# Weighted rows in two column tiles and whole scores behind each quarter, in a two-layer cross-attention

## The chip, the core and the metric

The kernel runs on one core of one Trainium2 chip. All arithmetic is in fp32. The metric is the device time in microseconds (us) of one execution, as the median of several. A profiled execution gives a page and a trace, in which times are microseconds from the start of its span and TensorE's clock is the share that was granted.

## What is computed

Two layers of cross-attention act on x (8 batches of 100 rows and 1024 features). The keys and values of both come from the same context (8 batches of 1444 rows of 512 features). Cut to what matters, the reference is:

```python
# layer 0, for each batch
Q, K, V = x @ Wq + bq, ctx @ Wk + bk, ctx @ Wv + bv
w = softmax(Q @ K.T / 32, axis=keys)        # 100 x 1444
x = x + (w @ V) @ Wo + bo
# layer 1, for each batch
q, k, v = x @ Wq + bq, ctx @ Wk + bk, ctx @ Wv + bv
w = softmax(q @ k.T / 32, axis=queries)     # 100 x 1444
z = w @ v + x
out = (z - mean(z)) / sqrt(var(z) + 1e-6) * gamma + beta
```

## The kernel before, in words

The products are regrouped. Instead of keys, the kernel forms the product of the query and key weights (`weight_products`), applies it to x (`queries`, giving gT: 512 context features by 400 columns for four batches) and multiplies by the context itself. Instead of values, it weights the context's rows first (`weighted_rows`) and applies the value weights afterwards (`project0`, `project1`, `project_last`). Many of the large products are done in Strassen-like form, with sums on the other engines.

For each batch of each layer there are then two products with the context:

- `scores` (line 921): 100 queries by 1444 context rows, with 512 features to sum over in `LC` = 4 chunks of 128. A chunk of gT (128 x 100) is the stationary operand, that of the transposed context `cT` (128 x 1444) moves. The result lies in `NB` = 4 PSUM banks. With `alone=True` the 1444 columns are cut into 4 pieces of 361 columns, one a bank; otherwise into `NP` = 11 pieces of 131 or 132, three to a bank. The function is a generator: each `next` issues one matmul, and the last of them also issues the evictions by ScalarE (line 945) and as much of the softmax as belongs there.
- `weighted_rows` (line 898): 512 context features by 100 queries, with the context rows to sum over in `MC` = 12 chunks of 120 (the last has 124). A chunk of context rows `c` by 128 features is the stationary operand, the chunk's weights `w` (120 x 100) move, and the four blocks of 128 features lie side by side in one PSUM bank of 400 columns. That is 48 calls a batch, with 4 for each chunk; each `next` issues one.

An fp32 matmul call appears in the trace as two weight loads (LDWEIGHTS, engine PEld) and two matmuls (engine PE).

`alternated` (line 1292) joins the two: for batch b it loads the rows of b in four parts and the features of b + 2 in four chunks, and then issues a step of A (the weighted rows of b) and one of s (the scores of b + 2) in turn, until both are used up: 48 of A and 44 of s. Batches 6 and 7 have no scores to run beside. The loads are issued by SP's queue, in order, into the `stream` pool of ten buffers; a buffer is filled again when its last reader has ended.

The order on TensorE is that of the program (`manual_schedule(engines={PE})`), so the main loops set it:

- Scores of batches 0 and 1 come alone in each layer (`first_scores`, 16 calls each).
- Layer 0 (loop at line 1310): batches 0 to 5 are alternated. In batches 6 and 7 parts of projection 0 (`o0`) are put in behind every fourth step of A.
- Layer 1 (loop at line 1374 and on): batches 0 to 7 in the sets 0 to 3, 4 to 6 and 7, with `project1` behind the first two. `finish` transposes finished rows back with one transpose behind a step of A, eight to a batch (`untransposed`, line 1183); the table `finished` starts it at steps 2, 16 and 30 of batch 4, 34 of batch 5, and 2, 15 and 28 of batch 7. `weight_totals` (line 1147) puts two transposes behind one step of batches 1, 3, 5 and 7.

The softmax of layer 0 runs along the rows and is then transposed on VectorE (16 STREAM_TRANSPOSE instructions); that of layer 1 transposes first and then takes maxima, exponentials and sums by groups of four chunks. Both make the weights `w` that A of the same batch reads, one batch later than the scores' own.

Of the kernel before, what the change touches and what calls it, by code (L numbers as in the profile page):

```python
# [29 lines left out]
PE = mybir.EngineType.PE  # L30

P = 128
B, T, E = 8, 100, 1024
S, L = 1444, 512
EC, LC = E // P, L // P
NQ = 4
MC, MR = 12, 120
MX = S - MC * MR
QR = MR * MC // NQ
CQ = MC // NQ  # L40
GM = 4
NP, PM = 11, 3
NB = -(-NP // PM)
QD = 32
SW = (MC - 1) * MR + P
PT = 4
# [9 lines left out]
def two_layer_cross_attention(ctx: ExitStack, tc: tile.TileContext, a: dict, out: bass.AP):  # L56
    nc = tc.nc
# [10 lines left out]
    def bank(name):  # L68
        return psum.tile([P, 512], F32, tag="ps", name=name)

    def bank2(name):
        return psum2.tile([P, 512], F32, tag="ps2", name=name)

    def unit(name):
        return stream.tile([P, E + L], F32, tag="unit", name=name)

    def wide(name):
        return work.tile([P, LC, GT], F32, tag="AT", name=name, bufs=2)

# [3 lines left out]
    def weight_rows(name):  # L83
        return work.tile([P, MC * T + QD * (-(-T // QD)) - T], F32, tag="wT", name=name, bufs=3)
# [35 lines left out]
    quarter = const.tile([P, P // QD], F32, tag="quarter", name="quarter")  # L120
# [747 lines left out]
    def load_features(b):  # L868

        for k in range(LC):  # L870
            t = unit(f"cT_{b}_{k}")[:, :S]
            nc.sync.dma_start(out=t, in_=a["ctxT"][b][k * P : (k + 1) * P, :])
            yield t

    def load_rows(b):

        src = a["ctx_512"][b]
        for q in range(NQ):
            t = unit(f"c_{b}_{q}").rearrange("p (c l) -> p c l", c=CQ)
            n = CQ - (q == NQ - 1)  # L880

            rows = bass.AP(src.tensor, src.offset + q * QR * L, [[L, P], [MR * L, n], [1, L]])
            nc.sync.dma_start(out=t[:, :n, :], in_=rows)
            if n < CQ:
                m = (MC - 1) * MR
                for r0, r1 in ((0, 112), (112, MR + MX)):
                    nc.sync.dma_start(out=t[r0:r1, n, :], in_=src[m + r0 : m + r1, :])
            yield t
# [5 lines left out]
    def held(c):  # L894

        return MR + (MX if c == MC - 1 else 0)

    def weighted_rows(w, c, dst, name):

        ps = bank2(name)  # L900
        for m in range(MC):
            r = held(m)
            for k in range(LC):
                nc.tensor.matmul(  # L904
                    ps[:, k * T : (k + 1) * T],
                    c[m // CQ][:r, m % CQ, k * P : (k + 1) * P],
                    w[:r, m, :],
                    start=(m == 0 and k == 0),
                    stop=(m == MC - 1),
                    skip_group_check=True,  # L910
                )
                if (m, k) == (MC - 1, LC - 1):
                    src = ps[:, :GT].rearrange("p (c t) -> p c t", t=T)
                    if name.startswith("A1"):
                        nc.scalar.copy(dst, src)
                    else:
                        nc.vector.tensor_copy(dst, src)
                yield


    def scores(s, layer, cT, softmax, alone=False):

        b = s["b"]
        p = s["p"] = prob[b % len(prob)][:T, :S]
        q = gT[layer][b // G]
        t0 = b % G * T
        n_pieces, per = (NB, 1) if alone else (NP, PM)
        cuts = [S * n // n_pieces for n in range(n_pieces + 1)]
        banks = [bank(f"s{layer}_{b}_{n}") for n in range(NB)]
        for k in range(LC):  # L930
            for n in range(n_pieces):
                o = cuts[n // per * per]
                nc.tensor.matmul(  # L933
                    banks[n // per][:T, cuts[n] - o : cuts[n + 1] - o],
                    q[:, k, t0 : t0 + T],
                    cT[k][:, cuts[n] : cuts[n + 1]],
                    start=(k == 0 and n % per == 0),
                    stop=(k == LC - 1),
                    skip_group_check=True,
                )  # L940
                if (k, n) != (LC - 1, n_pieces - 1):
                    yield
        parts = [slice(cuts[n * per], cuts[min((n + 1) * per, n_pieces)]) for n in range(NB)]
        for part, ps in zip(parts, banks):
            nc.scalar.activation(  # L945
                p[:, part],
                ps[:T, : part.stop - part.start],
                AF.Identity,
                bias=key_bias[layer][:T, b : b + 1],
                scale=SCALE,  # L950
            )
        w = s["rows"] = weight_rows(f"w{layer}_{b}")
        s["w"] = w[:, : MC * T].rearrange("p (c t) -> p c t", t=T)

        s["softmax"] = softmax(s, parts)
        for _ in islice(s["softmax"], LATER.get((layer, b))):
            pass
        yield
# [318 lines left out]
    batches = [{"b": b} for b in range(B)]  # L1277
    A0 = [wide(f"A0T_{g}") for g in range(2)]

    def loaded(*loads):  # L1280

        got = [[] for _ in loads]
        for _ in range(NQ):
            for load, to in zip(loads, got):
                to.append(next(load))
        return got
# [5 lines left out]
    def alternated(b, layer, softmax, dst):  # L1292

        nxt = b + 2 < B
        c, *cT = loaded(load_rows(b), *([load_features(b + 2)] if nxt else []))
        A = weighted_rows(batches[b]["w"], c, dst, f"A{layer}_{b}")
        ahead = scores(batches[b + 2], layer, *cT, softmax) if nxt else iter(())
        for _ in range(MC * LC):
            next(A)
            next(ahead, None)  # L1300
            yield

    key_bias = [c0, None]
# [6 lines left out]
    for b in range(B):  # L1310
        steps = alternated(b, 0, softmax0, A0[b // G][:, :, b % G * T : (b % G + 1) * T])
        if b == B - 2:
            o0 = project0(AS, A0)
        if b < B - 2:
            run(steps)
        else:

            more = next(o0)
            if b == B - 1:
                gT[1], queries1 = queries(1, wqk1, u1)  # L1320
            for n, _ in enumerate(steps):
                if n % 4 == 3 and n > 4:
                    next(more, None)
                    if b == B - 1 and n < 16:
                        next(queries1)
        for e in range(2 * b, 2 * b + 2) if 2 * b < EC else ():
            add_out_bias(e)
        if b == 0:
            sums = quarter_sums("k1")
            block_sums("u1", acc_u, sums[:, :LC, :], late=True)  # L1330
            block_sums("wqbk1", acc_c, sums[:, LC : LC + EC, :], late=True)
        if b == 1:
            got = totals("k1", sums[:, : LC + EC, :], LC + EC)
            u1, wqbk1 = got[:, :LC], got[:, LC:]
            vector.in_order = True
            AS = value_sums(wvo)
            vector.in_order = False
# [36 lines left out]
    for bs in SETS:  # L1374
        t = wide(f"A1T_{bs[0]}").rearrange("p c t -> p (c t)")[:, : LC * len(bs) * T]
        t = t.rearrange("p (c t) -> p c t", c=LC)
        for i, b in enumerate(bs):
            for n, _ in enumerate(alternated(b, 1, softmax1, t[:, :, i * T : (i + 1) * T])):
                if b % 2 and n == (8 if b == B - 1 else 27):
                    weight_totals(batches[b - 1 : b + 1])  # L1380
                if (b, n) in finished:
                    finishing.append(finish(batches[finished[b, n]]))
                finishing = [f for f in finishing if next(f, finishing) is not finishing]
            if b == 1:
                AS = project1_sums(wv1)
        if b == B - 2:
            first = last_columns(wv1)
        if b < B - 1:

            between, room = {3: (batches[5], (0, 3, 3, 3, 3)), 6: (batches[7], (1, 0, 0, 1, 2))}[b]  # L1390
            project1(bs, *AS, t, between["softmax"], room)
# [26 lines left out]
```

## Time and profile before

| | us |
|---|---|
| time, median of 2 runs | 632.83 (632.43 to 633.23) |
| profiled execution: span, which is the only time the page gives for it | 630.5 |
| busy: PE / PEld (of the span) | 621.6 (99%) / 534.7 (85%) |
| busy: DVE / ACT / POOL | 474.2 / 179.5 / 97.7 |
| A: matmul records / load records, 1536 of each | 249.8 / 218.0 busy |
| s of both layers: matmul records, 1184 | 245.6 busy |
| mean granted clock of TensorE | 0.997 |

PE's busy time counts the matmuls and PEld's the weight loads that overlap them. Records of consecutive matmuls overlap as well, since each is shown with its way through the array, so the busy time of a group is less than its count times its mean; the rate is read from the starts, or from the chain of waits, whose pieces do not overlap.

The stages in order of time: weight products and queries to 183; first scores to 203; layer 0's batches with scores to 321; its batches 6 and 7 to 350; projection 0, queries of layer 1 and its first scores to 436; layer 1's batches 0 to 3 to 515, `project1` to 534, batches 4 to 6 to 588, `project1` to 602, batch 7 and the end to 630.5.

### The profile page before, as it was taken

The page shows a single profiled execution, that of the slowest core. Times are in us where ns is not written, and L with a number is a line of the kernel's source. Part 1 is how long each engine was busy: PE and PEld are TensorE (multiplying, and loading weights), DVE is VectorE, ACT ScalarE, POOL GpSimd, SP SyncE. Part 2 cuts the span into 40 slices and gives each one's busy share as a digit, 9 for nine tenths or more (in the row PEclk, how much of TensorE's full clock was granted, in tenths as well). Part 3 has the DMA queues.
Part 4 walks back from the last instruction along what each step waited for, and adds up shares of the span by engine and source line. Part 5 has one row for each costly group of instructions (what it writes and reads, how often), then busy time and mean ns, then how long its engine had stood idle before and what let it go on. Part 6 is the DMA issues. An engine that isn't in the chain of part 4 may idle for free.

```text
span 630.5 us, 10617 instructions
## 1 busy us (share of the span) xinstructions
PE 621.6 (99%) x4142; PEld 534.7 (85%) x4142; DVE 474.2 (75%) x990; ACT 179.5 (28%) x406; POOL 97.7 (16%) x141
## 2 busy tenths in 40 slices
PE   9999999999999999999999999999999999999995
PEld 8886467688986999999989666756999999999992
DVE  2987688896875797666658686968777659887885
ACT  1323123314304234423230001113433240338303
POOL 3110111112230000000000002108111220423042
PEclk9999999999999999999999999999999999999998
DMA  8969989636999889998942309856889890697414
GB/s 273 295 147 320 306 220 333 120 80 117 206 326 388 269 311 293 329 313 313 298 161 86 104 0 337 268 195 192 298 298 309 309 315 26 198 289 282 124 24 83
DMA packets 54959, 144.35 MB, mean 229 GB/s; under 512 B 4732, under 2 KB 10108, under 8 KB 54908
## 3 DMA queue, kind: packets, MB, share of 16 engines
q1 hardware_dynamic: 46462, 119.63, 54.9%
q0 software_dynamic: 8048, 23.57, 17.9%
q8 instruction: 33, 0.54, 0.4%
q10 hardware_dynamic: 398, 0.47, 0.2%
q14 instruction: 18, 0.15, 0.1%
HBM read 123.36 MB, written 6.14 MB: 205 GB/s over the span
## 4 chain that ended last, share of the span: by engine, by line
PE 97%; issue 1%; ACT 0%; POOL 0%; DVE 0%; DVEq 0%; POOLq 0%; ACTq 0%
PE s L933 25%; PE A L904 25%; PE qk_x L163 7%; PE g_x L163 5%; PE o_x L163 5%; PE vo_x L163 3%; PE o_y L163 3%; PE g_y L163 3%; PE qk_y L163 2%; PE qk_z L163 2%; PE o_z L163 1%; PE o_w L163 1%; PE qk_w L163 1%; PE vo_y L163 1%; PE vo_z L163 1%; PE z L1198 1%
## 5 line engine op out<-in xcount | busy, mean ns | idle before, releaser
L904 PE MATMUL A<-w,c 120*128 120x100 f32 (+1 forms) x1536 | 249.8, 265 | 0.0
L904 PEld LDWEIGHTS A<-w,c 120*128 120x128 f32 (+1 forms) x1536 | 218.0, 190 | 2.8
L96 DVE STREAM_TRANSPOSE w<-prob 32x384 f32<-32x384 f32 (+1 forms) x256 | 143.7, 561 | 27.6 <-ACT prob L972 9.7
L933 PE MATMUL s<-cT,g1T 128*100 128x131 f32 (+2 forms) x592 | 122.9, 296 | 0.0
L933 PE MATMUL s<-cT,g0T 128*100 128x131 f32 (+2 forms) x592 | 122.7, 296 | 0.0
L933 PEld LDWEIGHTS s<-cT,g1T 128*100 128x100 f32 x592 | 78.4, 167 | 8.6 <-issue 0.3
L933 PEld LDWEIGHTS s<-cT,g0T 128*100 128x100 f32 x592 | 78.2, 167 | 8.4 <-PE c L599 0.4
L945 ACT ACTIVATE prob<-s,c 100x393 f32<-100x393 f32 (+2 forms) x64 | 34.7, 559 | 112.6 <-PE s L933 99.4
L1121 ACT ACTIVATE w<-w,negmax 120x100 f32<-120x100 f32 (+1 forms) x96 | 34.8, 365 | 82.6 <-DVE negmax L96 82.6
L965 DVE TENSOR_REDUCE maxima<-prob 100x1 f32<-100x394 f32 (+3 forms) x32 | 16.5, 528 | 24.3 <-ACT prob L945 24.0
L1362 POOL DMA_DIRECT2D wv<-in_L_xattn_Wv x1 | 0.8, 777 | 192.8 <-PE o_x L163 192.8
L163 PE MATMUL qk_x<-qk 128*128 128x256 f32 x128 | 30.0, 382 | 0.0
L1140 POOL TENSOR_TENSOR part<-w 120x500 f32<-120x500 f32 x8 | 10.9, 1366 | 118.5 <-DVE rstd L1213 28.6
L163 PEld LDWEIGHTS qk_x<-qk 128*128 128x128 f32 x128 | 23.6, 193 | 3.0 <-ACT qk L437 0.2
L675 ACT ACTIVATE g1T<-g_x,k 128x400 f32<-128x400 f32 x4 | 2.4, 594 | 68.9 <-PE g_x L163 68.7
L1121 ACT ACTIVATION_READ_ACCUMULATOR w<-w,negmax 120x1 f32 (+1 forms) x96 | 18.0, 187 | 0.0
L96 DVE TENSOR_TENSOR xT<-xT,o_x 128x400 f32<-128x400 f32 (+1 forms) x32 | 15.8, 538 | 2.2 <-PE o_x L163 2.0
L1202 DVE SCALAR_TENSOR_TENSOR z<-vectors,r,z 100x512 f32<-100x512 f32 x16 | 11.8, 740 | 6.3 <-PE z L1198 6.3
L1198 PE MATMUL z<-ident,xT 128*100 128x128 f32 x64 | 16.3, 273 | 0.0
L163 PE MATMUL vo_x<-vo 128*128 128x512 f32 x32 | 15.3, 595 | 0.0
L969 ACT ACTIVATE prob<-prob,negmax 100x1444 f32<-100x1444 f32 x8 | 12.0, 1498 | 11.2 <-DVE negmax L967 11.2
L96 DVE TENSOR_TENSOR w<-w,rtotal 120x400 f32<-120x400 f32 (+1 forms) x24 | 14.1, 586 | 0.7
(433 smaller groups left out, 987.8 us busy)
## 6 DMA issues: line engine op xcount, KB each, us to landing
cT<-in_ctxT SPq DMA_DIRECT2D x64, 722.0 KB, 6.8
c<-in_ctx SPq DMA_DIRECT2D x48, 768.0 KB, 7.6
c<-in_ctx SPq DMA_DIRECT2D x16, 512.0 KB, 8.0
vo<-in_L_xattn_Wo SPq DMA_DIRECT2D x8, 512.0 KB, 7.7
qk<-in_L_xattn_WqT SPq DMA_DIRECT2D x8, 512.0 KB
qk<-in_L_xattn_WqT SPq DMA_DIRECT2D x15, 256.0 KB, 5.8
c<-in_ctx SPq DMA_DIRECT2D x16, 224.0 KB, 6.4
xT<-in_xT SPq DMA_DIRECT2D x2, 1600.0 KB
```

Source lines behind the costliest of these rows:

```text
L96: ins = getattr(nc.vector, op)(*args, **kw)
L163: nc.tensor.matmul(banks[n // per][:, n % per * width : (n % per + 1) * width], lhs[i][:, n * P : (n + 1) * P], rhs[i], start=(fresh and i ...
L675: nc.scalar.activation(dst[g][:, c, :], banks[j][:, :GT], AF.Identity, bias=u[:, c : c + 1])
L904: nc.tensor.matmul(ps[:, k * T : (k + 1) * T], c[m // CQ][:r, m % CQ, k * P : (k + 1) * P], w[:r, m, :], start=(m == 0 and k == 0), stop=( ...
L933: nc.tensor.matmul(banks[n // per][:T, cuts[n] - o : cuts[n + 1] - o], q[:, k, t0 : t0 + T], cT[k][:, cuts[n] : cuts[n + 1]], start=(k == ...
L945: nc.scalar.activation(p[:, part], ps[:T, : part.stop - part.start], AF.Identity, bias=key_bias[layer][:T, b : b + 1], scale=SCALE,)
L965: nc.vector.tensor_reduce(maxima[:, n : n + 1], p[:, part], AX.X, ALU.max)
L969: nc.scalar.activation(p, p, AF.Exp, bias=negmax, accum_out=total)
L1121: nc.scalar.activation(w[:r, m0 + m, :], w[:r, m0 + m, :], AF.Exp, bias=negmax[:r, m : m + 1], accum_out=total[:r, m : m + 1])
L1140: add(part, w[:MR, 0:5, :], w[:MR, 5:10, :], ALU.add)
L1198: nc.tensor.transpose(ps[:T, e * P : (e + 1) * P], xT[:, 4 * j + e, b * T : (b + 1) * T], ident)
L1202: nc.vector.scalar_tensor_tensor(z[:, half], bv1[j][:T], s["r"], ps[:T, :], ALU.mult, ALU.add)
```

## The change

In `weighted_rows` each matmul of 128 features becomes two of 64. The first writes PSUM partitions 0 to 63 and the second 64 to 127 of the same columns, with the same moving operand. The columns of the array that a matmul uses follow the partitions that it writes, so the two are column tiles. The weighted rows have 96 calls a batch in place of 48; a `next` issues two.

In `alternated` the scores are taken with `alone=True` (16 calls of 361 columns in place of 44 of 131 or 132), and they are not issued one for each step of A: behind steps 11, 23, 35 and 47 come four calls, which are one feature chunk over all four pieces. The sixteenth `next` issues the last matmul, the evictions and the start of the softmax, at step 47; before, that came at step 43.

```diff
+HP = P // 2
...
         for m in range(MC):
             r = held(m)
             for k in range(LC):
-                nc.tensor.matmul(
-                    ps[:, k * T : (k + 1) * T],
-                    c[m // CQ][:r, m % CQ, k * P : (k + 1) * P],
-                    w[:r, m, :],
-                    start=(m == 0 and k == 0),
-                    stop=(m == MC - 1),
-                    skip_group_check=True,
-                )
+                for h in range(2):
+                    nc.tensor.matmul(
+                        ps[h * HP : (h + 1) * HP, k * T : (k + 1) * T],
+                        c[m // CQ][:r, m % CQ, k * P + h * HP : k * P + (h + 1) * HP],
+                        w[:r, m, :],
+                        start=(m == 0 and k == 0),
+                        stop=(m == MC - 1),
+                        skip_group_check=True,
+                    )
...
         A = weighted_rows(batches[b]["w"], c, dst, f"A{layer}_{b}")
-        ahead = scores(batches[b + 2], layer, *cT, softmax) if nxt else iter(())
-        for _ in range(MC * LC):
+        ahead = scores(batches[b + 2], layer, *cT, softmax, alone=True) if nxt else iter(())
+        quarter = MC * LC // NQ
+        for n in range(MC * LC):
             next(A)
-            next(ahead, None)
+            if n % quarter == quarter - 1:
+                for _ in range(NB):
+                    next(ahead, None)
             yield
```

## The prediction

> **What bounds the kernel now.** The page comes first: is one engine busy throughout, and does the chain that ended last run on it?
>
> ```profile
> span 630.5 us, 10617 instructions
> PE 621.6 (99%) x4142; PEld 534.7 (85%) x4142; DVE 474.2 (75%) x990; ACT 179.5 (28%) x406; POOL 97.7 (16%) x141
> ...
> PE 97%; issue 1%; ACT 0%; POOL 0%; DVE 0%; DVEq 0%; POOLq 0%; ACTq 0%
> ...
> L904 PE MATMUL A<-w,c 120*128 120x100 f32 (+1 forms) x1536 | 249.8, 265 | 0.0
> L904 PEld LDWEIGHTS A<-w,c 120*128 120x128 f32 (+1 forms) x1536 | 218.0, 190 | 2.8
> ```
>
> TensorE is the path: 97% of the chain, and no idle time before its matmuls. Every fp32 matmul of the program is two records (768 calls, 1536 records of A), each with its own weight load. A busy PE does not say whether matmuls or loads set the pace, so the next view is busy time by stage, over four batches of the weighted rows A with the scores s: two of layer 0, two of layer 1.
>
> ```profile
> core 0: us, PE busy (x) PEld busy (x) DVE busy (x) ACT busy (x) POOL busy (x), PEclk, DMA share, GB/s
> ...
> 262.40:282.10 19.70, 19.70 (x187) 19.70 (x186) 12.04 (x24) 7.04 (x9) 0.00 (x0) 1.00 0.94 322
> 282.10:301.70 19.60, 19.60 (x186) 19.60 (x185) 11.94 (x24) 7.04 (x9) 0.00 (x0) 1.00 0.90 302
> ...
> 476.00:495.60 19.60, 19.60 (x186) 19.60 (x185) 12.86 (x26) 7.16 (x30) 3.60 (x7) 1.00 0.92 314
> 495.60:515.30 19.70, 19.70 (x186) 19.70 (x185) 12.82 (x26) 7.07 (x29) 3.62 (x7) 1.00 0.89 301
> ```
>
> Matmuls and weight loads are both busy without a gap, at the full clock: a load runs while the matmul ahead of it streams, and the longer of the two sets each step. How long is a step? The timeline inside a batch:
>
> ```profile
> 539.66 0.36 PE L904 MATMUL A<-w,c 120*128 120x100 f32 x2
> 539.86 0.39 PE L933 MATMUL s<-cT,g1T 128*100 128x131 f32 x2
> 540.09 0.36 PE L904 MATMUL A<-w,c 120*128 120x100 f32 x2
> 540.28 0.39 PE L933 MATMUL s<-cT,g1T 128*100 128x131 f32 x2
> 540.51 0.36 PE L904 MATMUL A<-w,c 120*128 120x100 f32 x2
> ```
>
> A takes 0.20 us from its start to the next start, s 0.23, a pair 0.43. Last the chain of waits, where its pieces show both kinds alone and the steps that prices are taken from.
>
> ```profile
> 73.62 6.87 PE vo_x L163 x16
> ...
> 395.84 5.37 PE g_x L163 x16
> ...
> 426.62 9.73 PE s L933 x32
> ...
> 494.57 1.09 PE A L904 x10
> ...
> 576.35 11.59 PE A L904 x104
> ```
>
> A alone takes 0.111 a record (11.59/104), 0.222 a step. Matmuls whose moving side is wide follow their width: 400 columns 0.336 (5.37/16), 512 columns 0.429 (6.87/16), so 0.83 ns a column, and s in pieces of 361 columns 0.304 (9.73/32), as that slope gives. So 100 columns stream in 0.336 - 300 x 0.00083 = 0.087, and A alone, at 0.111, is held by the load of its 128 columns. In the pair, A's 0.20 is 0.111 for its own second load and 0.087 for the 100-column load of s. Loads of 128 and 100 columns in 0.111 and 0.087 give 0.056 for 64.
>
> **The change, part by part.** (1) *Scores in wide pieces.* Per batch 44 calls of 131 columns become 16 of 361: 32 records x 0.304 = 9.73 us. Their 0.087 loads hide behind 0.304 of streaming.
>
> (2) *Weighted rows in halves.* A step of two records becomes four, each with a 64-column load and the same 100 moving columns: the halves share neither. No row of this trace shows an output of 64 partitions or two matmuls in the array at once, so the step is bounded: 2 x 0.087 = 0.174 if both halves stream and load side by side; 4 x 0.087 = 0.348 if they go one after another; between them, 4 x 0.056 = 0.224 if the streams overlap and the loads stay in one file. I take 0.224, nearest to the row that sets A's pace today, a load queue that is never idle.
>
> Twelve batches have scores beside them (0 to 5 of each layer); each takes 19.63 now (by the chain: one ends at 262.44, the next at 282.07). New: 48 x 0.224 + 9.73 = 20.48, so +0.85 each, +10.2. Four batches are A alone: 4 x 48 x (0.224 - 0.222) = +0.4.
>
> (3) *Changes of the array's shape.* Scores, transposes and projections stay at full width, so every passage from halves to them or back is a change. Alternated batches: 2 layers x 6 x 4 quarters x 2 = 96. Layer 0, batches 6 and 7: the chain shows 8 and 7 insertions of projection 0, 30, and 2 at the ends. Layer 1: the transposes of `finish` follow single A steps; 24 in batch 4, two of them behind scores, 22 x 2 = 44; 8 in batch 5, one behind scores, 14; 24 in batch 7, 48; three weight totals between A steps, 6; entry and exit of batches 6 and 7, 4. In all 244. No row has such a change. The lower bound is 0 (a transpose between A steps costs 0.11 today, its load and nothing more). The upper is an emptied array and an uncovered load: an A matmul lasts 0.264 of which 0.087 is streaming, leaving 0.177; a load lasts 0.190 where 0.111 is its pace, so 0.079 + 0.056 = 0.135 for a half; together 0.31. I take 0.09, the middle of 0 and 0.177 with the load hidden: 244 x 0.09 = +22.0. The ends are 0 and +76.
>
> *Trainium skill, against this change.* The trace has loads running under matmuls of the same rows (19.70 of 19.70 busy on both). "TensorE: Matmul & The Clock Gate", Part 3, The mechanism, says that a load overlaps matmuls in flight only where its row group differs; two column halves have the same rows. By that rule a step would be 4 x (0.056 + 0.087) = 0.572 and the time 911; by the trace's rows it stays 0.224 and the sum below. "TensorEngine Tiling (Array Packing)", Overview and Key Properties, recommends tiles for dimensions of at most 64, where these are 128 features that fill the array, and says that a change of tiling mode drains TensorE; it gives no figure, and no row here shows one. The same page says tiles load and multiply in parallel, which would be the 0.174.
>
> (4) *What hides at nothing.* Scores end with the last A step, not 4 steps (0.9 us) before it, and the last eviction is 0.56, so the softmax starts 1.1 to 1.4 later. Its layer 1 chain, the longer:
>
> ```profile
> 475.57 9.46 DVE L96 STREAM_TRANSPOSE w<-prob 32x384 f32<-32x384 f32 x16 [4.15 <-POOL wsum L1145]
> ...
> 490.43 0.57 DVE L96 TENSOR_TENSOR w<-w,rtotal 124x400 f32<-124x400 f32 x1
> ```
>
> The weights are ready at 491.0 and A needs them at 495.4 (494.57 + 8 records): 4.4 of cover, 3.0 after the shift, 1.5 if batches also shrink by 1.5. Uncovered, it would cost its excess in each of 12 batches. SP's queue issues the same DMAs in the same order. A row tile is freed up to 2.4 earlier (a quarter's scores now come behind it), a feature tile at 25, 50, 75 and 100% of the batch against 23, 46, 69 and 92%; the ten-buffer rotation reuses each about one batch before it is read, 19.6 against 6.8 to 8 us to landing. POOL's queue is not touched. The four score banks are now taken at the first scores call, n = 11, not n = 0, when those before have been evicted.
>
> **Sum.** 630.5 + 10.2 + 0.4 + 22.0 = 663.1 of span. The page gives no time beside its span; the median of the two runs is 632.83, 2.3 above it, and I add that: 665.
>
> **The rivals.** *Side by side and free (the other side).* Step 0.174: 12 x (8.35 + 9.73 - 19.63) = -18.6; A alone 192 x -0.048 = -9.2; each of the 122 runs of A starts and ends with one half alone, 122 x 0.087 = +10.6. Sum -17.2: 615.6 with free changes. For it: halves share no column and no partition of the result. Against: 218 us of A's loads in one unbroken file. It is faster only while a change costs under 17.2 / 244 = 0.07; over 2% only under 0.02. *Side by side, changes at 0.02 to 0.12, or loads in file and changes nearly free:* 620 to 645 (the latter 643 at 0). *One after another.* That is the case in which the change does not do what it says: step 0.348, 12 x 6.80 + 192 x 0.126 = +105.8, so 739 with free changes, 761 at 0.09, 783 at 0.177. For it: in every row of the trace matmuls start no closer than their stream or load allows. Against: each half uses other columns. *Softmax late* adds at most its excess and needs 3 us more; no time of its own.
>
> **How the numbers follow.** Two per cent, 12.7 us, is about what a measurement of this kernel can tell from no change: 620.2 and 645.5. Side by side and free (615 to 620) 0.18; cheap changes (620 to 645) 0.19; the forecast with changes at 0.01 to 0.23 (646 to 700) 0.37; one after another (739 to 783) 0.23; still dearer 0.03. Faster 0.18, same 0.19, slower 0.63. The forecast's own range is 646 to 700; the eight in ten reach from 615 to 760, leaving out the dearer half of the serial case, the 0.03 and a little below.
>
> **What would show it.** Step (1): 32 s records of 0.30 in a batch. Step (2): starts of A inside a quarter, 12 steps in 2.1, 2.7 or 4.2 us. Step (3): the time between the last A and the first s of a quarter over what their streams need, and the same at a transpose. Step (4): no wait of A for w. The prediction is wrong if the step lies below 0.2 or above 0.25, or a change outside 0 to 0.23.

## The result, and the profile after

The changed kernel takes 641.88 us (641.67 to 642.1, 2 runs) against 632.83: a ratio of 1.0145, 95% interval 1.0129 to 1.0162. The profiled execution spans 639.9 us, 9.4 more than before. It is slower, as forecast, but by 9 us and not by 32; by the two per cent that the prediction takes as its measure it counts as no change, though the interval is clear of 1. The page after, first the busy times, then the chain that ended last and the groups of A:

```profile
span 639.9 us, 12346 instructions
PE 630.7 (99%) x5006; PEld 451.8 (71%) x5006; DVE 476.2 (74%) x990; ACT 180.0 (28%) x406; POOL 98.7 (15%) x141
...
PE 77%; issue 8%; DVE 6%; ACT 4%; POOL 4%; POOLq 0%; DVEq 0%; ACTq 0%
...
L906 PEld LDWEIGHTS A<-w,c 120*64 120x64 f32 (+1 forms) x3072 | 135.2, 137 | 39.1 <-issue 26.3
L906 PE MATMUL A<-w,c 120*64 120x100 f32 (+1 forms) x3072 | 159.0, 253 | 0.3 <-issue 0.3
```

TensorE is still busy throughout. The chain that ended last gives it less (77%, before 97%): from 493 us on it is followed back over the softmax and the normalisations, with one piece of 26.9 us in which the engine waited for nothing that the profile shows, so it does not tell what bounds the kernel there. TensorE's own waits do. They are 1.7 us in all, one of them in A:

```profile
PE warm L109 <- DVE ones L106: 1.1, 1, 1.1
PE g_z_x L164 <- DVE qk L97: 0.3, 1, 0.3
PE A L906 <- issue: 0.3, 1, 0.3
```

But A's matmuls, twice as many, are busy for 159 us and not 250, and the weight loads are no longer one file without a gap (71%, before 85%). So A itself became much faster, and something else took the time back. Which stage? Busy time by stage, after:

```profile
203.26:319.05 115.79, 115.79 (x1348) 80.44 (x1347) 84.38 (x167) 38.86 (x51) 0.00 (x0) 1.00 0.93 316
319.05:348.72 29.67, 29.67 (x416) 21.43 (x415) 20.87 (x45) 3.71 (x5) 0.00 (x0) 1.00 0.25 79
...
531.97:591.76 59.79, 59.46 (x675) 39.99 (x675) 42.12 (x79) 23.73 (x71) 17.00 (x22) 1.00 0.73 228
...
606.31:624.57 18.26, 18.26 (x221) 12.20 (x221) 12.06 (x20) 2.34 (x3) 5.68 (x8) 1.00 0.15 23
```

and the same stages of the kernel before:

```profile
202.98:321.32 118.34, 118.34 (x1111) 118.34 (x1110) 84.61 (x169) 39.55 (x52) 0.00 (x0) 1.00 0.89 304
321.32:350.32 29.00, 29.00 (x222) 26.67 (x221) 20.09 (x43) 3.09 (x3) 0.00 (x0) 1.00 0.30 96
...
534.26:587.94 53.68, 53.68 (x500) 53.68 (x500) 45.30 (x84) 23.70 (x71) 16.71 (x22) 1.00 0.80 254
...
602.25:615.28 13.03, 13.03 (x125) 13.03 (x124) 11.14 (x20) 1.15 (x1) 5.53 (x8) 1.00 0.22 33
```

Layer 0's batches with scores gained 2.55 us, its batches 6 and 7 lost 0.67, layer 1's batches 0 to 3 gained 0.85 (78.94 to 78.09). The loss is in two stages, batches 4 to 6 of layer 1 (+6.11) and batch 7 (+5.23): those with the transposes of `finish` between steps of A. The rest of the span differs by 0.8 in all. Inside a batch of layer 0, the timeline after:

```profile
266.05 2.28 PE L906 MATMUL A<-w,c 120*64 120x100 f32 x48
268.26 2.68 PE L935 MATMUL s<-cT,g0T 128*100 128x361 f32 x8
270.87 2.28 PE L906 MATMUL A<-w,c 120*64 120x100 f32 x48
273.08 2.68 PE L935 MATMUL s<-cT,g0T 128*100 128x361 f32 x8
275.69 2.28 PE L906 MATMUL A<-w,c 120*64 120x100 f32 x48
```

A quarter is 2.21 us of A (from its start to that of s) and 2.61 of s, 4.82 together and 19.28 a batch; before, 19.63. Where transposes stand between single steps, the timeline after and then the one before, both from batch 7:

```profile
606.91 0.32 PE L1200 MATMUL z<-ident,xT 128*100 128x128 f32 x1
607.16 0.39 PE L906 MATMUL A<-w,c 120*64 120x100 f32 x4
607.48 0.32 PE L1200 MATMUL z<-ident,xT 128*100 128x128 f32 x1
```

```profile
602.74 0.28 PE L1198 MATMUL z<-ident,xT 128*100 128x128 f32 x1
602.85 0.36 PE L904 MATMUL A<-w,c 120*128 120x100 f32 x2
603.05 0.27 PE L1198 MATMUL z<-ident,xT 128*100 128x128 f32 x1
```

A transpose and a step of A take 0.57 where they took 0.31.

What the halves do is seen in single starts. The trace does not name the half of a record; that is read from the order and the spacing of the starts. It has, in microseconds, at the start of the first run of A above and around the scores ahead of it:

```
A, two records at a time  266.186 266.192   266.271 266.278   266.357 266.364   ... 86 ns from pair to pair
last pair of a run        263.256 263.263
load for s                263.441    second record of s 263.826, so the first streams from about 263.522
last record of s          265.654    it streams to about 265.958
loads of the next A       266.047 266.054    second pair 266.186, so the first streams from about 266.100
```

Two records start 6 to 7 ns apart, every 86 ns: 0.172 a step, the stream of 100 columns and nothing else. I take the two to be of different halves, since records of one half start 86 ns apart ("Half by half", below). And at a change of shape nothing is loaded for 0.09 us after the last stream has ended (0.088 to 0.092 at all 93 edges between A and scores), and then a load that was hidden lies open (0.08 for 100 columns, 0.05 for 64). A run of A costs its steps and two changes: 2.21 - 12 x 0.172 = 0.15 and 2.61 - 8 x 0.304 = 0.18, 0.32 with rounding.

### The profile page after: what moved, and what is told of

The parts are those of the page before. It is cut to its first block, busy times and chain, and to the rows that moved or that the text cites. A ratio compares the mean times of both kernels' runs of the same rounds, so it can differ in the third digit from the quotient of the medians.

```text
span 639.9 us, 12346 instructions
## 1 busy us (share of the span) xinstructions
PE 630.7 (99%) x5006; PEld 451.8 (71%) x5006; DVE 476.2 (74%) x990; ACT 180.0 (28%) x406; POOL 98.7 (15%) x141
## 4 chain that ended last, share of the span: by engine, by line
PE 77%; issue 8%; DVE 6%; ACT 4%; POOL 4%; POOLq 0%; DVEq 0%; ACTq 0%
PE s L935 21%; PE A L906 15%; PE qk_x L164 7%; PE g_x L164 5%; DVE w L97 5%; PE vo_x L164 3%; PE o_x L164 3%; PE g_y L164 3%; PE qk_z L164 2%; PE qk_y L164 2%; POOL rstd L1216 1%; PE o_y L164 1%; ACT z L1218 1%; ACT w L1123 1%; PE qk_w L164 1%
## 5 line engine op out<-in xcount | busy, mean ns | idle before, releaser
L906 PEld LDWEIGHTS A<-w,c 120*64 120x64 f32 (+1 forms) x3072 | 135.2, 137 | 39.1 <-issue 26.3
L906 PE MATMUL A<-w,c 120*64 120x100 f32 (+1 forms) x3072 | 159.0, 253 | 0.3 <-issue 0.3
L935 PE MATMUL s<-cT,g1T 128*100 128x361 f32 x256 | 84.2, 474 | 0.0
L935 PE MATMUL s<-cT,g0T 128*100 128x361 f32 x256 | 84.1, 474 | 0.0
L947 ACT ACTIVATE prob<-s,c 100x361 f32<-100x361 f32 x64 | 34.4, 561 | 104.8 <-PE s L935 90.4
L935 PEld LDWEIGHTS s<-cT,g1T 128*100 128x100 f32 x256 | 40.5, 166 | 31.5 <-issue 0.3
L935 PEld LDWEIGHTS s<-cT,g0T 128*100 128x100 f32 x256 | 40.3, 166 | 31.3 <-PE c L600 0.4
L967 DVE TENSOR_REDUCE maxima<-prob 100x1 f32<-100x361 f32 x32 | 16.4, 527 | 11.3 <-ACT prob L947 9.9
L1218 ACT ACTIVATE z<-z,rstd 100x1024 f32<-100x1024 f32 x7 | 8.0, 1149 | 30.2 <-POOL rstd L1216 30.2
L1216 POOL TENSOR_TENSOR rstd<-rstd,mhalf 100x1 f32<-100x1 f32 x7 | 9.8, 1393 | 43.1 <-DVE rstd L1215 43.1
```

Source lines behind the costliest of these rows:

```text
L906: nc.tensor.matmul(ps[h * HP : (h + 1) * HP, k * T : (k + 1) * T], c[m // CQ][:r, m % CQ, k * P + h * HP : k * P + (h + 1) * HP], w[:r, m, :],
L935: nc.tensor.matmul(banks[n // per][:T, cuts[n] - o : cuts[n + 1] - o], q[:, k, t0 : t0 + T], cT[k][:, cuts[n] : cuts[n + 1]], start=(k == ...
L947: nc.scalar.activation(p[:, part], ps[:T, : part.stop - part.start], AF.Identity, bias=key_bias[layer][:T, b : b + 1], scale=SCALE,)
L967: nc.vector.tensor_reduce(maxima[:, n : n + 1], p[:, part], AX.X, ALU.max)
L1216: nc.gpsimd.tensor_tensor(rstd, rstd, mhalf[:T], ALU.pow)
L1218: nc.scalar.activation(z, z, AF.Copy, scale=rstd)
```

## The experiments

Each kernel starts from the changed one, and the code shown is shortened where it has `...`. Theory 1 is that the halves run side by side and each change between them and full width costs; the rivals are named in each expectation. Ratios are to the kernel before, on the same chip. A difference from the changed kernel's 641.9 compares two measurements; beside them the kernel before took 632.4 to 632.8.

**Weighted rows whole, blocks kept.** The loop over `h` is taken out again.

```diff
-                for h in range(2):
-                    nc.tensor.matmul(ps[h * HP : (h + 1) * HP, ...], c[...][:r, m % CQ, k * P + h * HP : ...], ...)
+                nc.tensor.matmul(ps[:, ...], c[...][:r, m % CQ, k * P : (k + 1) * P], ...)
```

> Weighted rows whole (128 features, as before the change), scores still in four wide pieces behind every quarter. Theory 1 (changing the shape of the array costs 0.29 us for each run of halves, which between changes take 0.174 a step): no change of shape is left, a step of A is 0.222 by its load, so 12 x (48 x 0.222 + 9.73 - 19.63) = +9 on the kernel before: about 642, and the last s and the first A of a quarter 0.30 apart. Theory 2 (the edges of the blocks cost, whatever the width of A): 48 edges x 0.29 on top, about 656.

Measured: 640.95, ratio 1.0132 (1.0116 to 1.0147). The chain of waits has A and s alone at the price of their steps:

```profile
277.69 2.44 PE s L934 x8
280.12 2.66 PE A L905 x24
282.78 2.44 PE s L934 x8
```

2.66 is 12 x 0.222 and 2.44 is 8 x 0.304: with one shape the edge of a block costs nothing. Theory 1 holds. The blocks without the halves are 8.5 us slower than the alternation, because A alone waits for its loads; the halves take that away and pay it back at the changes.

**Halves, alternation kept.** The other part is undone.

```diff
-        ahead = scores(batches[b + 2], layer, *cT, softmax, alone=True) if nxt else iter(())
+        ahead = scores(batches[b + 2], layer, *cT, softmax) if nxt else iter(())
...
             next(A)
-            if n % quarter == quarter - 1:
-                for _ in range(NB):
-                    next(ahead, None)
+            next(ahead, None)
```

> Weighted rows in halves, but the alternation of before (one step of A, one narrow piece of s). Theory 1 (each run of halves costs 0.29 on top of its steps): a pair takes 0.174 + 0.29 + 0.224 = 0.69 in place of 0.43, 44 pairs x 12 batches x 0.26 = +138, with the transposes and the last batch some 775. Theory 2 (a run of halves loses only the half that has no partner, 0.087; nothing is emptied): +0.058 a pair, about 668.

Measured: 790.43, ratio 1.2494 (1.2469 to 1.2519). Its chain of waits:

```profile
276.20 0.40 PE s L935 x2
276.60 0.32 PE A L906 x4
276.93 0.40 PE s L935 x2
```

A pair takes 0.72: 0.172 + 0.15 and 0.224 + 0.18. Theory 1, with a change slightly dearer than expected.

**Two blocks of scores a batch in place of four.**

```diff
-        quarter = MC * LC // NQ
+        half = MC * LC // 2
...
-            if n % quarter == quarter - 1:
-                for _ in range(NB):
+            if n % half == half - 1:
+                for _ in range(2 * NB):
```

> As the changed kernel, with two blocks of eight calls of s per batch in place of four of four. Theory 1 (0.29 for each run of halves): 24 runs fewer, -7.0, about 635. Theory 2 (the loss lies in the transposes alone, or in what a step costs): no difference, 642.

Measured: 634.0, ratio 1.0023 (1.0013 to 1.0033). That is 7.9 less. The trace has 100 runs of A in place of 122: 22 fewer and not 24, since two transposes that stood behind scores now stand alone. So 0.36 each. The chain of waits leaves the rest of the kernel out:

```profile
278.77 4.27 PE A L906 x96
283.05 5.04 PE s L935 x16
```

9.31, where two quarters took 9.64: 0.33 for the run that is gone. Theory 1.

**The transposes of a finished batch in one go.**

```diff
-    finished = {(4, 2): 0, (4, 16): 1, (4, 30): 2, (5, 34): 3, (7, 2): 4, (7, 15): 5, (7, 28): 6}
+    finished = {(4, 11): 0, (4, 23): 1, (4, 35): 2, (5, 35): 3, (7, 8): 4, (7, 19): 5, (7, 30): 6}
...
-                if b % 2 and n == (8 if b == B - 1 else 27):
+                if b % 2 and n == (8 if b == B - 1 else 35):
...
-                    finishing.append(finish(batches[finished[b, n]]))
-                finishing = [f for f in finishing if next(f, finishing) is not finishing]
+                    run(finish(batches[finished[b, n]]))
```

> As the changed kernel, with the eight transposes of each finished batch in one go, behind the scores of a quarter where there are any (batches 4 and 5) and three times in batch 7; the weight totals too. Theory 1 (0.29 for each run of halves): 53 runs fewer, -15, about 627. Theory 2 (a transpose itself takes 0.25 in this kernel, wherever it stands): 642. If the eight wait for the eviction of their two banks, up to 1 us for each of the seven comes back.

Measured: 631.34, ratio 0.9979 (0.9969 to 0.9988), 10.5 below the changed kernel. So it is not the transpose itself. For 53 runs that is 0.20 each, less than elsewhere. The waits of TensorE have part of what is missing to 627:

```profile
PE z L1200 <- DVE r L1156: 2.3, 1, 2.3
...
PE ol L1260 <- ACT A1T L917: 0.9, 1, 0.9
PE A L906 <- issue: 0.8, 1, 0.8
```

The transposes of batch 3 wait until VectorE has read the weight totals (`r`), which now stand right before them. With these 4.0 us a run costs 0.27; the rest stays open.

**Half by half.** Within a chunk the loop over `h` is put outside that over `k`; a `next` still issues two calls.

```diff
-            for k in range(LC):
-                for h in range(2):
+            for h in range(2):
+                for k in range(LC):
```

> As the changed kernel, but within a chunk of rows all four blocks of the lower half come first and then all four of the upper half. Theory 1 (matmuls start in program order, so only neighbours in different halves overlap): 14 of the 16 records of a chunk follow one another at 0.087, 1.22 + a little in place of 0.70 a chunk; 16 batches x 12 x 0.52 = +100, about 742. Theory 2 (the engine reorders over its queue, the order of the halves does not matter): 642.

Measured: 689.03, ratio 1.0888 (1.0866 to 1.0910): neither. In the trace's starts a group of eight records of one half (8 x 0.086 = 0.69) begins every 0.40 us, as at 274.255 and 274.655, while the group ahead, earlier in the program, still starts records at 274.335, 274.421 and 274.507. So matmuls of the two halves do start out of program order, which the strict form of theory 1 excluded, but not over any distance: a group starts when the fifth record of the eight ahead of it does (274.249), and 0.69/0.40 = 1.7 halves stream on average, not 2.

**Fifty queries.** From the second chunk on only 50 of the 100 queries are summed; that part of the weighted rows is left out.

```diff
-                        ps[h * HP : (h + 1) * HP, k * T : (k + 1) * T],
+                        ps[h * HP : (h + 1) * HP, k * T : k * T + (T if m == 0 else T // 2)],
...
-                        w[:r, m, :],
+                        w[:r, m, : (T if m == 0 else T // 2)],
```

> As the changed kernel, but of the weighted rows only 50 of the 100 queries are computed from the second chunk on (the rest of the sum is left out for the other 50). Streams halve to 0.0435, the loads stay. Theory 1 (the loads of the two halves run side by side, each about 0.056): a step falls from 0.174 to 0.11, 704 x 0.06 = -43, about 598. Theory 2 (loads come one after another, at 0.0435 each, and set the 0.174): no difference, 642.

Measured: 608.39, ratio 0.9614 (0.9595 to 0.9633). The timeline of a quarter:

```profile
271.09 1.61 PE L906 MATMUL A<-w,c 120*64 120x50 f32 x48
272.62 2.68 PE L935 MATMUL s<-cT,g0T 128*100 128x361 f32 x8
```

The trace's pairs start every 0.058 (271.240, 271.298, 271.356): four loads of 64 columns in 0.117, two at a time. In one file at the 0.056 estimated for each they would need 0.224, and the two loads of a pair start 7 ns apart (271.254 and 271.260). The loads of the halves run side by side. A step takes 0.117 and not 0.11, which is 5 of the 10 us over 598; TensorE also waits 2.8 once for VectorE's sums `k_sums`, with a granted clock of 0.50 for 3.4 us behind it, and 2.0 for nothing that the profile shows.

**Scores in tiles too.** Each scores call becomes two, of 64 and 36 queries.

```diff
-                nc.tensor.matmul(banks[n // per][:T, ...], q[:, k, t0 : t0 + T], ...)
+                for r0, r1 in ((0, HP), (HP, T)):
+                    nc.tensor.matmul(banks[n // per][r0:r1, ...], q[:, k, t0 + r0 : t0 + r1], ...)
```

> As the changed kernel, with the scores in column tiles too (64 and 36 queries), so that A and s have one shape and only the transposes, projections and totals differ. Theory 1 (the change of shape is what costs): 96 changes go, and with what the halves' unlike lengths (0.304 and 0.087) lose where s and A meet, about 0.13 for each of 48 blocks, -8 remain: about 634. Theory 2 (the blocks' edges cost in any shape): 642 or above.

Measured: 630.5, ratio 0.9961 (0.9947 to 0.9976). Its chain of waits has the quarter at 4.50 where the changed kernel has 4.82:

```profile
270.10 2.44 PE s L936 x16
272.54 2.06 PE A L906 x48
```

2.06 is 12 x 0.172 and 2.44 is 8 x 0.304. The edge costs nothing once both sides have one shape, not even the 0.13 allowed for unlike halves. That is 0.32 for each of 48 quarters, 15.4; the time fell by 11.4. The transposes behind scores, which changed no shape before, now do, and TensorE waits 1.2 for VectorE's `o_t`; what else comes back was not followed.

**Alternation, all in tiles.** The alternation of before, with both products in tiles.

> The alternation of before (one step of A, one narrow piece of s), with both in column tiles. If the change of shape is what the alternated halves paid (790), none is left between A and s: a pair takes 0.172 + 2 x 0.11, 12 x 0.1 more than the blocks of scores in tiles: about 632. If it is the alternation as such, or the narrow pieces, or their loads: near 790, or between.

Measured: 632.16, ratio 0.9995 (0.9984 to 1.0005), where the halves alternated with whole scores took 790. The 158 us between these two are changes of shape: 528 pairs at 0.72 and at 0.40 differ by 169, and 11 come back where 32 transposes and three pairs of weight totals stand next to scores, which is a change only when the scores are in tiles (35 x 0.32).

**Four tiles of 32 features.** `range(4)` and a quarter of the features each.

> As the changed kernel, with four column tiles of 32 features in place of two of 64. Theory 1 (starts in order, and of the two records of each call only the second can overlap the first of the next tile): four calls take 4 x 0.087 a step whatever the number of tiles, 0.35, so 768 x 0.174 = +134, about 776. Theory 2 (all tiles stream together): at most 642.

Measured: 650.98, ratio 1.0287 (1.0266 to 1.0307). Theory 1 as written here fails: 96 records take what 48 took,

```profile
271.75 2.27 PE L906 MATMUL A<-w,c 120*32 120x100 f32 x96
273.94 2.68 PE L935 MATMUL s<-cT,g0T 128*100 128x361 f32 x8
```

2.19 for 12 steps. All four tiles stream together, by starts out of program order. That is theory 2, yet the time is 9 us over it. TensorE stops four times in A for nothing that the profile shows, 6.9 in all, most of it in batch 6 of layer 1, which has no scores:

```profile
591.42 3.07 PE L906 MATMUL A<-w,c 120*32 120x100 f32 x127 [3.02 <-issue]
597.61 3.21 PE L906 MATMUL A<-w,c 120*32 120x100 f32 x67 [3.12 <-issue]
600.75 3.65 PE L164 MATMUL o_x<-A1T,wv 128*128 128x150 f32 x16
```

```profile
596.69:603.52 6.83, 5.91 (x78) 5.62 (x79) 1.89 (x8) 0.49 (x1) 0.00 (x0) 0.50 0.01 2
```

The first matmuls of `o_x` are slow because the granted clock is 0.50 for 6.8 us from 596.69 on, in which TensorE is busy for 5.9: some 3 us more. With the two stops shown that is the 9. Such a run has twice the instructions for each microsecond. The supply of instructions would explain the stops, and each of the two has one transfer of 16 KB on the queue that the page calls `instruction` in it (at 589.08 and 595.17); no run here tests that, and it stays open.

**Combined, whole scores in two blocks.** Two blocks, transposes grouped, weight totals at step 23, and projection 0 put in in two groups a batch.

> Halves for A, scores whole in two blocks per batch, the eight transposes of a finished batch in one go, the weight totals at step 23, the insertions of projection 0 in two groups a batch. By the cost of a run of halves (0.3 us): 24 runs fewer by the blocks, some 49 by the transposes and totals, 11 by the projection, 84 x 0.3 = -25 on the changed kernel: about 617. If the grouped transposes or projections wait for evictions, up to 5 us of it comes back.

Measured: 623.4, ratio 0.9859 (0.9842 to 0.9876); 6.4 over. The profiled execution, at 625.4 the longest of the four, has waits of TensorE of 2.6 (for xT) and 2.3 (for o_t), both on VectorE, and a granted clock of 0.50 for 6.8 us behind the first.

**Combined, one shape.** Scores in tiles, four blocks, the rest grouped in the same way.

> Scores in column tiles like A (64 and 36 queries), so that A and s have one shape, four blocks per batch as in the change; transposes, totals and projections grouped. From the 630.5 of scores in tiles: 50 changes of the transposes at 0.3 and 11 of the projection, -18: about 613, faster than the kernel before by 3%. If the changes cost only where scores are involved: 630.

Measured: 621.77, ratio 0.9828 (0.9815 to 0.9841). Faster than the kernel before, but 9 short of 613. The longest waits of TensorE, and its stages around the longer of them, which lasts from 574.50 to 577.96 (the number ahead of the last two is the granted clock):

```profile
PE o_y L164 <- DVE o_t L97: 3.4, 1, 3.4
PE o_z_x L164 <- DVE xT L97: 2.7, 1, 2.7
```

```profile
574.50:576.86 2.36, 0.04 (x1) 0.00 (x0) 2.26 (x5) 0.00 (x0) 0.00 (x0) 1.00 0.46 170
576.86:583.69 6.83, 5.73 (x23) 5.73 (x24) 6.25 (x19) 2.94 (x17) 0.00 (x0) 0.50 0.00 0
583.69:584.94 1.25, 1.25 (x12) 1.25 (x11) 0.31 (x1) 1.25 (x8) 0.00 (x0) 1.00 0.00 0
```

A faster TensorE catches up with VectorE. And the 3.4 us of idle cost more than themselves: 2.4 us into them the granted clock falls to 0.50 for 6.83 us, and the first 16 matmuls behind take 4.16 in place of 2.04. In these 6.83 us TensorE is busy for 5.73, half of it lost: 2.9. The two waits and this are 9.0, about what is missing to 613.

**Its waits taken up.** The last kernel, but for these places (the code is shown against the changed kernel):

```diff
-                if n % 4 == 3 and n > 4:
-                    next(more, None)
...
+                if n % 12 == 11:
+                    for _ in range(2 if n < 47 else 3):
+                        next(more, None)
...
-    finished = {..., (5, 34): 3, ...}
+    finished = {..., (5, 11): 3, ...}
```

> As the version with one shape and grouped transposes, with its two waits of TensorE taken up: the inner products of projection 0 go in two at a time behind every twelfth step, so that each eviction has a group of A steps to end in, and batch 3's transposes stand a half batch earlier, which takes about 4 us of VectorE's work away from before the second projection of layer 1. If the two waits (2.7 and 3.4) and the slow stretch behind the second (4.2 and 2.8 for what took 2.2 each) were what held it at 622: 622 - 2.7 - 3.4 - 2.6 + 4 x 0.3 for four more changes = about 614. If the transposes' grouping itself cost that, and the waits are only where it shows: 620 or above.

Measured: 617.9, ratio 0.9767 (0.9754 to 0.9781), the fastest here. Both waits are gone; the weight totals have a new one, `PE wsum_ps L1155 <- DVE z L1205: 2.4, 1, 2.4`, since batch 3's rows now stand on VectorE just before them, and the clock is 0.50 for 3.4 us behind it.

## Why the prediction was wrong, point by point

- **What bounds the kernel: right.** A waited for its 128-column loads, TensorE was the path and stayed it (1.7 us of waits after).
- **Step (1), wide pieces: right.** 8 records in 2.44 within a block, nothing exposed where the shape is one.
- **Step (2), the halves: this is the step that failed.** It took 0.224 a step, with the loads in one file, "nearest to the row that sets A's pace today". Measured: 0.172, below the 0.2 that the prediction itself named as a sign that it is wrong. The fifty-query run shows the reason: loads of different halves run side by side, at 0.058 a pair. The 0.056 for one load was right; that the four follow one another was not. The row of unbroken loads showed one load path for one full-width array and could say nothing of two tiles. In the sum, 12 x (48 x 0.172 + 9.73 - 19.63) + 192 x (0.172 - 0.222) = -19.7 - 9.6 = -29.3 stands where +10.6 stood.
- **Step (3), the changes: right in kind and count, too small in price.** The trace has the 122 runs of A that were counted. At 0.32, as read from the quarters, they are +39.0; it had 244 x 0.09 = +22.0. The bounds held (0 to 0.31 a change; 0.16 measured), the 0.09 taken as a middle happens to be what the empty stretch alone costs, and the next load, which the choice left hidden, lies open for 0.05 to 0.08 more. Alternated halves (0.33 a run), two blocks (0.33) and scores in tiles (0.32) confirm this term; grouped transposes show its kind, at 0.20 to 0.27.
- **Step (4), nothing hidden fails: right.** TensorE's three waits are for no weights and no scores bank; the one in A, 0.3 us, is for nothing named.
- **The sum.** 630.5 - 29.3 + 39.0 = 640.2 for a measured span of 639.9; so close is partly luck, since by stages the same sum is up to 0.8 off, either way. The two errors, -40 and +17, partly cancel, so that the direction came out right with the wrong size.
- **The rivals.** "Side by side" was the mechanism. Its 10.6 us for a half alone at each end of a run does not exist, since the halves start 6 to 7 ns apart, and its cheap changes do not either. That 641.9 lies among the times given to it (620 to 645) is luck: changes dearer than its 0.12, less the 10.6. "One after another" fell (its 783 is 782 by its own terms).

The two pages weighed against each other in the prediction are settled by these runs. The Trainium skill, "TensorE: Matmul & The Clock Gate", Part 3, The mechanism, says that a load overlaps matmuls in flight only where row groups differ (another sentence of that section adds loads into a background weight buffer); here loads of two halves of the same rows run beside each other and under matmuls, 0.172 a step where that rule gives 0.572. "TensorEngine Tiling (Array Packing)", Key Properties, says that tiles load and multiply in parallel and that a change of tiling mode drains the engine; both agree with the trace, which adds the price: 0.09 us without a load, and the next load in the open. That page, Overview, names dimensions of at most 64 as the ones to tile and so misses this case: the features fill the array, and tiles still gain 0.05 a step because a load of 128 columns was longer than a stream of 100.

## What to carry to other kernels

Here a stationary operand took longer to load (0.111 us) than the moving one to stream (0.087), and two column tiles took the load off the path. Where that may hold, count every passage between tile shapes on that engine, at about 0.16 us each by these runs, before the steps. Here 53 transposes between single steps and 48 blocks of scores ate the whole gain; giving the neighbours the same shape and grouping the transposes returns it (617.9 against 632.5). A faster engine then meets the next one's lateness, and idle time of TensorE can be paid again in the clock behind it.

## What the runs showed of the hardware that was not expected

- Matmuls of different column tiles start out of program order: in the half-by-half run three earlier records start after a later one, and with four tiles 16 records take 0.172 a step. In the changed kernel two records start 7 ns apart at the head of a run, read as one of each half, where the program has both records of the lower half first. The Trainium skill, "TensorE: Matmul & The Clock Gate", Part 3, The mechanism, has matmuls in strict program order; the trace differs. The distance is limited: a group of eight records started with the fifth of the eight ahead of it, 1.7 tiles streaming and not 2.
- Four tiles of 32 columns, with 100 moving columns each, stream together at 0.086 us a record: 16 loads and matmuls in 0.172.
- A gap of 3.4 us on TensorE brought the granted clock to 0.50, 2.4 us after it began, for 6.8 us. Waits of 2.4, 2.6, 2.8 and 3.1 in other runs were followed by 3.4 or 6.8 us at 0.50 as well; waits of 2.3, 2.7 and 3.0 were not. So the length of the wait alone does not tell which.
